# A four-stage transformer kernel on one core: five edits to its small elementwise steps and PSUM banks, with new order tables

## The chip, the cores and the metric

The kernel runs on one NeuronCore of a Trainium2 chip. A core has five engines with a queue each: PE (TensorE, matrix products; its weight loads are shown apart as PEld), DVE (VectorE), ACT (ScalarE), POOL (GpSimd) and SP, which here only issues DMAs. PE writes to PSUM, eight banks of 128 x 512 float32 values; DVE and ACT read PSUM and SBUF; POOL is used here on SBUF alone. The metric is device time in microseconds (us) of one execution, the median of several runs. Each engine works through its own instructions strictly in order and waits on semaphores, so an instruction that waits holds up all that stand behind it on that engine.

## The reference, cut to what matters

The input x is 16 blocks (batch elements) of 256 tokens by 128 features, with a context of 64 tokens per block. Four layers follow each other, each as x = x + tanh(gate) * layer(layernorm(x)):

```python
x = x + tanh(g_xattn[0]) * cross_attention_0(layernorm(x), ctx)   # 16 heads of 8, causal and padding masks
x = x + tanh(g_ffn[0])   * local_ffn(layernorm(x))                # 2 deep: windowed attention (8 heads of 64,
                                                                  # l2-normed q and k, rotary) and a gated MLP of 341
x = x + tanh(g_xattn[1]) * cross_attention_1(layernorm(x), ctx)   # 16 heads of 8, biases, padding mask
x = x + tanh(g_ffn[1])   * experts(layernorm(x))                  # 8 experts of width 128 or 256, top 2 by sigmoid
```

In the windowed attention the score of query i with key j is divided by both norms; the softmax subtracts the row maximum. In the experts every expert is computed for every token, and y = sum over e of comb[e] * y_e, with comb zero but for the best two. All is float32 but some masks.

## The kernel before

**Stages.** The program has three parts. `cross(0)` runs the first cross-attention over blocks 0 to 15, together with one-time preparation (transposing weights, keys and values of the context, masks). `local_ffn` runs for each depth l = 0, 1 the windowed attention over all blocks and then the gated MLP (GLU) over all blocks. `cross(1)` and `experts` run last, the experts beginning while the second cross-attention drains. A block is two tiles of 128 tokens; steps with a digit (top0, top1) are done once per tile, j = 0, 1.

**What sets the order.** Each stream is a table of steps (CROSS_STEPS, LOCAL_STEPS and so on), one line per step: name, lag in blocks, engine, cost, steps it needs, PSUM bank or buffer it takes and who gives that back. `timetable` (L337) walks the streams with the costs and emits one global order, which is then each engine's fixed order; earlier streams have priority. The costs are only the planner's; the chip follows the order at its own speed. A class of banks can have several homes: BIG means any of BIG0, BIG1, BIG2 (two banks each), while M and O are one bank each (`anywhere`, L1672).

**Cross-attention, one block.** DVE takes the statistics (`stat`), POOL the inverse root (`rstd`), DVE an offset -mean*rstd (`offset`, L926), POOL applies both (`apply`, L932). PE then turns the result (`turn`, bank M), makes the query (`query`, M), the scores (`score`, BIG); DVE takes row maxima (`top`) and splits them into bf16 parts (`parts`); PE turns those (`mturn`, M), makes the transposed scores (`score_t`, BIG); ACT does the exponentials (`exp`); PE mixes values (`mix`, bank O, L1103); ACT and DVE form the inverse sums (`log`, `inverse`, `refine`) and `share`, which gives O back; PE projects (`project`, M) and DVE adds to x (`add`, L1146), which gives M back.

**Windowed attention, one tile.** PE: `hturn` (bank VB), `qk` (QK, L1254), `value` (VB). ACT squares, DVE does `sin`, `cos` (both L1268, from PSUM) and `sums`. POOL: `clip`, `rotate` (two adds, L1302 and L1303), `norm` (four small operations), `scale` (L1330), `share` (L1400). PE turns q and k (bank TR), scores (bank SC, one tile at a time); DVE `top` takes the negated row maxima (L1373) and multiplies them by the query norms (L1378, 128 x 8); ACT `exp` does eight activations with that as bias (L1387) and gives SC back; DVE `total`, POOL `share`, PE `pturn` and `mix`. In layer 0 a further stream, `first`, normalizes blocks 2 to 15 with the same stat, rstd, offset, apply (writing y_sb) beside the attention.

**Experts, one block.** PE makes hidden units in three parts (`hid0` to `hid2`, L1623), ACT relu and square, PE the outputs of all 8 experts for one tile of tokens, `out0` and `out1` (L1645, 24 matmul records each, one BIG home each). DVE `sum` (L1653) adds the eight weighted outputs one after the other into x_sb, which gives the BIG home back, and SP stores the tile.

**Start.** Weights 0 (Wk), 1 (Wq), 2 (Wv), 3 (Wo) of the first cross-attention come by DMA, 0 and 1 on ACT's queue, 2 and 3 on SP's (L478 to L496). `wturn0` turns 0 and 1, `wturn1` turns 2 and 3 (L693).

Of the kernel before, what the change touches and what calls it, by code (L numbers as in the profile page):

```python
# [12 lines left out]
BF16 = mybir.dt.bfloat16  # L13
# [27 lines left out]
rstd 3 POOL 1.03 stat  # L41
mix 5 PE 1.8 exp0,exp1,vals O:share
query 2 PE 0.6 turn_out M:query_out
score_t 4 PE 1.2 mturn_out,query_out,keys BIG:exp0 BIG:exp1
share 6 DVE 0.43 refine oT:project
turn_out 3 ACT 0.38 turn xnT:query
log 6 ACT 0.38 mix
stat 0 DVE 0.92 - sm:apply
top0 3 DVE 1.2 score
project 6 PE 0.5 share M:add  # L50
query_out 3 ACT 0.39 query QT:score+score_t
inverse 6 ACT 0.38 log
top1 3 DVE 1.2 score,top0
parts 3 DVE 0.9 top0,top1 mp:mturn
add 6 DVE 0.48 project
exp0 5 ACT 1.08 score_t pT:mix
vals 5 POOL 0.32 - V:mix
apply 3 POOL 1.02 offset xn:turn
mturn 3 PE 0.25 parts M:mturn_out
offset 0 DVE 0.16 rstd  # L60
exp1 5 ACT 1.08 score_t,exp0
score 2 PE 1.25 query_out,keys BIG:top0 BIG:top1
turn 1 PE 0.4 apply M:turn_out
mturn_out 4 ACT 0.38 mturn mT:score_t
refine 5 DVE 0.84 inverse
keys 4 POOL 0.6 - Kd:score+score_t
# [3 lines left out]
inverse 6 ACT 0.38 log  # L70
score 6 PE 1.25 query_out,keys BIG:top0 BIG:top1
apply 1 POOL 1.02 offset xn:turn
stat 3 DVE 0.92 - sm:apply
turn 5 PE 0.4 apply M:turn_out
top0 6 DVE 1.2 score
exp0 5 ACT 1.08 score_t pT:mix
mturn_out 4 ACT 0.38 mturn mT:score_t
exp1 5 ACT 1.08 score_t,exp0
mix 8 PE 1.8 exp0,exp1,vals O:share
rstd 0 POOL 1.03 stat  # L80
top1 6 DVE 1.2 score,top0
parts 6 DVE 0.9 top0,top1 mp:mturn
keys 0 POOL 0.6 - Kd:score+score_t
query 5 PE 0.6 turn_out M:query_out
offset 4 DVE 0.16 rstd
add 9 DVE 0.48 project
turn_out 2 ACT 0.38 turn xnT:query
score_t 7 PE 1.2 mturn_out,query_out,keys BIG:exp0 BIG:exp1
refine 8 DVE 0.84 inverse
share 8 DVE 0.43 refine oT:project  # L90
log 5 ACT 0.38 mix
vals 2 POOL 0.32 - V:mix
project 9 PE 0.5 share M:add
query_out 2 ACT 0.39 query QT:score+score_t
mturn 6 PE 0.25 parts M:mturn_out
# [3 lines left out]
hid2 4 PE 1.88 turn_out,hid1 BIG:relu2  # L99
stat 4 DVE 0.92 -  # L100
hid0 3 PE 1.88 turn_out BIG:relu0
prob 8 ACT 0.22 router
rstd 0 POOL 0.95 stat
apply 0 POOL 0.9 offset exn:turn
relu1 7 ACT 1.06 hid1,relu0
out0 5 PE 2.9 square0,square1,square2 BIG:sum0
turn_out 6 ACT 0.38 turn exnT:hid2+router
square0 7 ACT 1.04 relu0
sum1 8 DVE 1.95 out1,route
router 4 PE 0.45 turn_out O:prob  # L110
relu2 7 ACT 1.06 hid2,relu1
sum0 7 DVE 1.95 out0,route
out1 5 PE 2.9 square0,square1,square2 BIG:sum1
square2 7 ACT 1.04 relu2
square1 7 ACT 1.04 relu1
offset 4 DVE 0.16 rstd
route 6 DVE 2.7 prob cb:sum0+sum1
hid1 3 PE 1.88 turn_out,hid0 BIG:relu1
relu0 6 ACT 1.06 hid0 h:out0+out1
turn 2 PE 0.44 apply M:turn_out  # L120
# [3 lines left out]
FIRST_STEPS = """  # L124
vals_out1 8 DVE 0.7 vals1
wturn_out1 4 ACT 0.38 wturn1
wturn1 4 PE 0.4 wload1 BIG:wturn_out1
vals2 8 PE 1.0 vals1,cdup1 BIG:vals_out2
dve 2 LD 1.4 -
vals_out2 9 DVE 0.7 vals2  # L130
wturn_out0 1 ACT 0.38 wturn0
unit 6 ACT 1.6 narrow
mload0 4 LM 5.0 -
cdup1 3 DVE 0.69 cturn1
pturn 5 PE 0.3 pens BIG:pturn_out
cdup0 4 DVE 0.69 cturn0
keys1 8 PE 0.95 cturn_out1 BIG:keys_out1
pool 8 LP 4.6 -
narrow 2 DVE 0.21 dve
cload0 0 LC 5.0 -  # L140
heads 1 DVE 0.62 dve
gates 5 ACT 0.3 act
nload 2 LN 8.0 -
act 9 LA 3.2 -
cturn1 1 PE 0.7 cload1 BIG:cturn_out1+cdup1
cturn_out1 5 ACT 0.61 cturn1
vals1 5 PE 1.0 vals0 BIG:vals_out1
xload0 3 LX 4.1 -
keys0 4 PE 1.7 wturn_out0,cturn_out0 BIG:keys_out0
wturn0 0 PE 0.8 wload0 BIG:wturn_out0  # L150
vals_out3 8 DVE 0.7 vals3
cload1 1 LC 2.2 cload0
cturn_out0 1 ACT 0.61 cturn0
part 2 DVE 0.55 dve
mload1 5 LM 6.0 mload0
pturn_out 5 DVE 0.2 pturn
late 2 DVE 2.0 pool
vals0 4 PE 1.1 wturn_out1,cdup0 BIG:vals_out0
keys_out0 5 ACT 0.61 keys0
wload0 3 LW 5.0 -  # L160
xload1 7 LX 1.5 xload0
wload1 6 LW 2.6 wload0
fill1 6 DVE 0.65 mload1,fill0
sels 3 DVE 0.28 heads
cturn0 0 PE 1.0 cload0 BIG:cturn_out0+cdup0
fill0 3 DVE 0.28 part,mload0
pens 4 DVE 0.7 nload
vals3 8 PE 1.0 vals2 BIG:vals_out3
keys_out1 9 ACT 0.61 keys1
vals_out0 4 DVE 0.7 vals0  # L170
# [3 lines left out]
keys1 1 PE 0.95 wturn_out BIG:keys_out1  # L174
vals_out0 6 DVE 0.7 vals0
bias 3 DVE 0.25 cols_out
vals1 4 PE 0.98 wturn_out BIG:vals_out1
wturn_out 4 ACT 0.62 wturn
rw_out 7 DVE 0.2 rw
cols_out 1 DVE 0.35 cols  # L180
cols 0 PE 0.15 - BIG:cols_out
vals_out3 2 DVE 0.7 vals3
vals0 4 PE 0.98 wturn_out BIG:vals_out0
rw 6 PE 0.15 - BIG:rw_out
keys_out1 1 DVE 0.75 keys1,cols_out
bo 2 PE 0.4 bias,wturn_out BIG:bo_out
vals_out1 4 DVE 0.7 vals1
keys_out0 8 DVE 0.75 keys0,cols_out
bo_out 4 DVE 0.25 bo
keys0 7 PE 0.95 wturn_out BIG:keys_out0  # L190
vals_out2 8 DVE 0.7 vals2
vals3 1 PE 0.98 wturn_out BIG:vals_out3
vals2 7 PE 0.98 wturn_out BIG:vals_out2
wturn 0 PE 0.6 - BIG:wturn_out
# [3 lines left out]
tab1 2 DVE 0.5 -  # L198
local2 7 POOL 0.65 -
tab2 8 DVE 0.5 -  # L200
seen 0 DVE 1.0 -
fill 0 DVE 1.2 -
local0 1 POOL 0.98 -
tab3 3 DVE 0.5 -
local1 8 POOL 0.65 -
local3 3 POOL 0.8 -
tab0 0 DVE 0.5 -
# [3 lines left out]
stat 0 DVE 0.92 -  # L211
rstd 0 POOL 0.95 stat
offset 1 DVE 0.16 rstd
apply 1 POOL 0.9 offset
# [9 lines left out]
norm0 3 POOL 0.87 root0  # L224
mix0 5 PE 1.07 pturn_out0,dma0 OB:mix_out0
qk1 2 PE 1.75 hout QK:square1+sin1+cos1
hout 0 ACT 0.78 hturn hb:qk0+qk1+value0+value1
sin1 2 DVE 1.21 qk1 u:rotate1
value0 3 PE 0.911 hout VB:value_out0
pturn0 4 PE 1 share0 TR:pturn_out0  # L230
share1 5 POOL 1.9 total1
mix1 5 PE 1.07 pturn_out1,dma1,dma0 OB:mix_out1
pturn_out1 4 ACT 1.02 pturn1 pT:mix1
mix_out0 4 ACT 0.62 mix0 oT:project
value_out0 3 DVE 0.7 value0 v:mix0+mix1
exp1 3 ACT 2.6 top1 pr:pturn1
total1 4 DVE 1.4 exp1
top0 3 DVE 1.4 score0,norm0
score0 3 PE 1.24 turn_out0 SC:exp0+top0
cos1 2 DVE 1.21 qk1 qn:turn1  # L240
root0 1 ACT 0.45 clip0
pturn_out0 3 ACT 1.02 pturn0 pT:mix0
dma1 7 DMA1 2.5 value_out1
sums1 2 DVE 1.22 square1
scale0 3 POOL 1.05 rotate0,norm0
clip1 3 POOL 0.27 sums1
square1 1 ACT 1.04 qk1 sq:sums1
turn1 3 PE 0.995 scale1 TR:turn_out1
mix_out1 4 ACT 0.62 mix1,mix_out0
rotate1 3 POOL 2.56 sin1,cos1  # L250
value1 3 PE 0.911 hout VB:value_out1
value_out1 3 DVE 0.7 value1
share0 4 POOL 1.9 total0
turn_out1 2 ACT 1.02 turn1
add 5 DVE 0.42 project
project 5 PE 1.69 mix_out0,mix_out1 OB:add
exp0 2 ACT 2.6 top0 pr:pturn0
total0 3 DVE 1.4 exp0
sin0 1 DVE 1.21 qk0 u:rotate0
cos0 1 DVE 1.21 qk0 qn:turn0  # L260
qk0 1 PE 1.75 hout QK:square0+sin0+cos0
turn0 2 PE 0.995 scale0 TR:turn_out0
square0 0 ACT 1.04 qk0 sq:sums0
norm1 3 POOL 0.87 root1
turn_out0 1 ACT 1.02 turn0 qT:score0+score1
scale1 3 POOL 1.05 rotate1,norm1
hturn 0 PE 0.3 - VB:hout
clip0 2 POOL 0.27 sums0
top1 3 DVE 1.4 score1,norm1
score1 3 PE 1.24 turn_out1,turn_out0 SC:exp1+top1  # L270
pturn1 4 PE 1 share1 TR:pturn_out1
root1 1 ACT 0.45 clip1
sums0 1 DVE 1.22 square0
dma0 0 DMA0 2.5 value_out0
rotate0 2 POOL 2.56 sin0,cos0
"""
GLU_STEPS = """
up0 1 PE 0.96 affine A:gate0+gate1
gelu2 2 ACT 0.47 up2,gelu0
bias 6 POOL 0.5 shift  # L280
shift 5 DMA2 2.8 - hg:apply
up1 1 PE 0.96 affine,up0
gate2 4 DVE 0.48 gelu2,gate0
gelu0 1 ACT 0.47 up0 hh:down
rstd 3 POOL 0.95 stat
stat 0 DVE 0.92 shift
gate0 3 DVE 0.48 gelu0
gelu1 1 ACT 0.47 up1,gelu0
out 4 DVE 0.48 down,bias
gate1 3 DVE 0.48 gelu1,gate0  # L290
down 2 PE 1.45 gate0,gate1,gate2
nturn 0 PE 0.44 apply N:affine
affine 0 ACT 0.5 nturn hnT:up0+up1+up2
apply 0 DVE 0.6 rstd hn:nturn
up2 1 PE 0.95 affine B:out
"""
LAST_GLU_STEPS = """
gate2 7 DVE 0.48 gelu2,gate0
apply 4 DVE 0.6 rstd hn:nturn
rstd 7 POOL 0.95 stat  # L300
shift 0 DMA3 2.8 - hg:apply
up0 4 PE 0.96 affine A:gate0+gate1
gate0 6 DVE 0.48 gelu0
back 8 DVE 0.35 out
bias 8 POOL 0.5 shift
gelu2 4 ACT 0.47 up2,gelu0
down 5 PE 1.45 gate0,gate1,gate2
up1 4 PE 0.96 affine,up0
out 7 DVE 0.48 down,bias
up2 4 PE 0.95 affine B:out  # L310
stat 3 DVE 0.92 shift
affine 2 ACT 0.5 nturn hnT:up0+up1+up2
gelu0 3 ACT 0.47 up0 hh:down
nturn 2 PE 0.44 apply N:affine
gelu1 3 ACT 0.47 up1,gelu0
gate1 6 DVE 0.48 gelu1,gate0
"""

LOGS, GELUS = "natural_log_exp_and_others", "gelu_and_others"

LOCAL_ROOM = dict(
    sq=1, u=2, qn=2, pr=2, pT=2, oT=2, qT=2, v=3, hb=3, hg=2, hn=2, hnT=2, hh=2,
    QK=1, SC=1, TR=1, VB=1, OB=1,
)
CROSS_ROOM = dict(
# [1443 lines left out]
```

## Time and profile before

| | |
|---|---|
| median of 3 runs | 1169.5 us (1165.39 to 1172.19) |
| the profiled execution | 1167.54 us, of which the span from first to last instruction is 1165.8 |
| granted TensorE clock | 0.986 of full speed |
| busy: PE, DVE, ACT, POOL | 1071.5, 938.5, 747.2, 631.9 us |
| HBM read, written | 9.46 MB, 2.10 MB |

By stage, from the trace's stretches (us busy in the stretch):

| stretch, us | what runs | length | PE | DVE | ACT | POOL |
|---|---|---|---|---|---|---|
| 30 to 147 | cross-attention 0 | 117 | 106.58 | 92.03 | 59.06 | 41.64 |
| 147 to 210 | windowed attention 0 fills | 63 | 45.94 | 51.68 | 37.04 | 48.58 |
| 210 to 390 | windowed attention 0 | 180 | 177.73 | 171.13 | 155.07 | 161.59 |
| 390 to 545 | its end, GLU 0, attention 1 fills | 155 | 135.69 | 111.16 | 89.27 | 75.65 |
| 545 to 750 | windowed attention 1 | 205 | 204.61 | 190.75 | 180.27 | 169.44 |
| 750 to 870 | its end, GLU 1, cross-attention 1 fills | 120 | 104.57 | 82.64 | 51.35 | 47.09 |
| 870 to 962 | cross-attention 1 | 92 | 82.75 | 75.51 | 55.12 | 48.65 |
| 962 to 1157.1 | experts | 195.1 | 194.83 | 138.65 | 108.54 | 24.46 |

How to read it: where PE is busy for all of a stretch, only less PE work or a faster PE shortens it; where PE has gaps, the waits say who closed each gap last. A busy engine is not proof of a bound, since a stretched instruction counts as busy too.

### The profile page before, as it was taken

Reading aid. Unit: us, or ns where it says so; the run is one execution under the profiler, and the core shown is the slowest. Engines: PE = TensorE matmul, PEld = TensorE weight load, DVE = VectorE, ACT = ScalarE, POOL = GpSimd, SP = SyncE. Lnnn points to the kernel's source line nnn. Section 1 sums busy time; section 2 is a strip of 40 time slices with the busy share of each in tenths; the row PEclk is TensorE's granted clock in tenths of the full one; section 3 lists DMA queues with packets and bytes.
Section 4 is the critical chain, followed back from the end, with each engine's and each line's share of the span. In section 5 each row is a group of like instructions: output and inputs, shape, how many; then the busy total and the mean of one; then the engine's idle time right before and its main releaser. Section 6 shows DMA issues by size and latency. Waiting matters only on the chain.

```text
span 1165.8 us, 29177 instructions
## 1 busy us (share of the span) xinstructions
PE 1071.5 (92%) x11648; PEld 802.7 (69%) x11648; DVE 938.5 (81%) x2088; ACT 747.2 (64%) x1465; POOL 631.9 (54%) x1047
## 2 busy tenths in 40 slices
PE   6999967999999989988999999979979999999997
PEld 4555625777777767855777777768745557999996
DVE  6887669999999965669999999857857884777777
ACT  3555437888888863458888888853336557555552
POOL 4453068999988843338888888733345460111110
PEclk9999979999999999999999999999989999999999
DMA  6400000111101111101111111111100000000000
GB/s 175 153 3 2 2 9 20 29 29 24 29 20 29 29 40 25 24 1 28 29 29 29 24 29 25 35 31 25 23 1 2 2 2 2 12 13 12 13 12 17
DMA packets 42740, 30.21 MB, mean 26 GB/s; under 512 B 21546, under 2 KB 35564, under 8 KB 42604
## 3 DMA queue, kind: packets, MB, share of 16 engines
q1 hardware_dynamic: 41260, 27.69, 9.5%
q8 instruction: 92, 1.51, 0.6%
q10 hardware_dynamic: 1344, 0.66, 0.2%
q14 instruction: 44, 0.36, 0.1%
HBM read 9.46 MB, written 2.10 MB: 10 GB/s over the span
## 4 chain that ended last, share of the span: by engine, by line
PE 64%; DVE 10%; DMA 4%; ACT 3%; issue 2%; SPq 2%; POOL 1%; DVEq 0%; POOLq 0%; ACTq 0%
PE QK L1257 9%; PE e_y L1645 7%; PE e_h_ps L1623 7%; PE OB L1417 5%; DMA gbuf<-y_sb 4%; PE TR L1405 4%; PE SC L1364 4%; PE TR L1336 4%; PE VB L1287 4%; PE OB L1436 3%; PE Ag L1515 3%; PE po L1111 2%; DVE qn L1268 2%; PE Bg L1515 2%; PE SC L1351 2%
## 5 line engine op out<-in xcount | busy, mean ns | idle before, releaser
L1387 ACT ACTIVATE pr<-SC,mx,rn 128x128 f32<-128x128 f32 x512 | 185.6, 469 | 23.5 <-DVE mx L1378 18.8
L1257 PE MATMUL QK<-wqkv,hbuf 128*128 128x512 f32 x256 | 129.4, 629 | 23.7 <-DVE qn L1268 22.8
L1400 POOL TENSOR_TENSOR pr<-pr,rs 128x1024 f32<-128x1024 f32 x64 | 121.5, 1899 | 10.5 <-DVE rs L1395 9.4
L1653 DVE SCALAR_TENSOR_TENSOR x_sb<-e_y,e_comb,x_sb 128x128 f32<-128x128 f32 x256 | 89.1, 349 | 21.6 <-PE e_y L1645 13.7
L1635 ACT ACTIVATE e_h<-e_h_ps 128x1024 f32<-128x1024 f32 x48 | 49.2, 1025 | 77.2 <-PE e_y L1645 61.8
L1268 DVE TENSOR_TENSOR u<-QK,tab 128x1024 f32<-128x1024 f32 x64 | 77.5, 1211 | 23.0 <-ACT sq L1265 13.8
L1645 PE MATMUL e_y<-mw,e_h 128*128 128x128 f32 x768 | 91.8, 277 | 0.0
L1623 PE MATMUL e_h_ps<-e_xnT,mw 128*128 128x256 f32 x384 | 89.8, 383 | 0.3
L1645 PEld LDWEIGHTS e_y<-mw,e_h 128*128 128x128 f32 x768 | 89.2, 192 | 0.7
L1257 PEld LDWEIGHTS QK<-wqkv,hbuf 128*128 128x128 f32 x256 | 44.4, 193 | 64.8 <-issue 43.9
L1373 DVE TENSOR_REDUCE mx<-SC 128x8 f32<-128x1024 f32 x64 | 77.5, 1212 | 12.1 <-PE SC L1364 12.1
L1036 DVE TENSOR_REDUCE nm<-sc 128x16 f32<-128x1024 f32 x64 | 74.8, 1210 | 14.0 <-PE sc L1027 13.8
L1302 POOL TENSOR_TENSOR qn<-qn,u 128x512 f32<-128x512 f32 x64 | 81.7, 1276 | 5.1
L1265 ACT ACTIVATE sq<-QK 128x1024 f32<-128x1024 f32 x64 | 65.7, 1026 | 26.3 <-ACT pr L1387 11.4
L1394 DVE TENSOR_REDUCE rs<-pr 128x8 f32<-128x1024 f32 x64 | 77.4, 1210 | 5.9 <-ACT pr L1387 4.1
L1303 POOL TENSOR_TENSOR qn<-qn,u 128x512 f32<-128x512 f32 x64 | 81.8, 1278 | 0.0
L1098 ACT ACTIVATE xpT<-sT,penT 128x1024 f32<-128x1024 f32 x64 | 69.5, 1114 | 17.5 <-PE sT L1088 17.4
L1268 DVE TENSOR_TENSOR qn<-QK,tab 128x1024 f32<-128x1024 f32 x64 | 77.6, 1213 | 1.1 <-ACT sq L1265 1.1
L1408 ACT COPY pT<-TR 128x1024 f32<-128x1024 f32 x64 | 64.4, 1006 | 21.6 <-PE TR L1405 21.6
L1623 PEld LDWEIGHTS e_h_ps<-e_xnT,mw 128*128 128x128 f32 x384 | 70.4, 190 | 10.9 <-DVE x_sb L1653 2.7
L1339 ACT COPY qkbuf<-TR 128x1024 f32<-128x1024 f32 x64 | 64.8, 1012 | 19.7 <-PE TR L1336 19.6
L1282 DVE TENSOR_REDUCE ss<-sq 128x16 f32<-128x1024 f32 x64 | 77.1, 1205 | 0.0
(213 smaller groups left out, 2629.1 us busy)
## 6 DMA issues: line engine op xcount, KB each, us to landing
vbuf<-vbuf SPq DMA_DIRECT2D x96, 128.0 KB
gbuf<-y_sb SPq DMA_DIRECT2D x32, 64.0 KB
out_dram<-x_sb SPq DMA_DIRECT2D x32, 64.0 KB
gbuf<-y_sb SPq DMA_DIRECT2D x32, 63.5 KB
wqkv<-in_L_ffn_wqkv_dram SPq DMA_DIRECT2D x2, 768.0 KB
mw<-in_L_ffn_w_dram SPq DMA_DIRECT2D x2, 768.0 KB
w<-in_L_ffn_w_dram SPq DMA_DIRECT2D x2, 341.0 KB
x_sb<-in_x_dram SPq DMA_DIRECT2D x1, 640.0 KB
```

The source lines that it names most:

```text
L1257: nc.tensor.matmul(ps[:, 512 * j : 512 * j + 512], lhsT=hbuf[b % 3][:, t * P : (t + 1) * P], rhs=wqkv[:, l, 512 * j : 512 * j + 512], star ...
L1268: nc.vector.tensor_tensor(work(tag, b, t, [P, 2, LH, LD], 2, wp), live["QK", b, t].rearrange("p (q h d) -> p q h d", q=2, h=LH), tab[:, l, ...
L1282: nc.vector.tensor_reduce(ss, live["sq", b, t].rearrange("p (g d) -> p g d", d=LD), AX.X, ALU.add)
L1302: nc.gpsimd.tensor_add(qg[:, :, 0:32], qg[:, :, 0:32], ug[:, :, 32:64])
L1303: nc.gpsimd.tensor_add(qg[:, :, 32:64], qg[:, :, 32:64], ug[:, :, 0:32])
L1373: nc.vector.tensor_reduce(mx, live["SC", b, t].rearrange("p (g c) -> p g c", c=P), AX.X, ALU.max, negate=True,)
L1387: nc.scalar.activation(pr[:, g, :], live["SC", b, t][:, g * P : (g + 1) * P], AF.Exp, bias=live["mx", b, t][:, g : g + 1], scale=live["rn" ...
L1394: nc.vector.tensor_reduce(rs, live["pr", b, t], AX.X, ALU.add)
L1400: nc.gpsimd.tensor_tensor(pr, pr, rs, ALU.mult)
L1623: nc.tensor.matmul(ps[:, c * S : (c + 1) * S], lhsT=mw1[:, (4 * j + c) * P : (4 * j + c + 1) * P], rhs=live["xnT", b], start=True, stop=True,)
L1645: nc.tensor.matmul(y[:, e * D : (e + 1) * D], lhsT=live["h", b][:, c, t * P : (t + 1) * P], rhs=mw2[:, c, :], start=(c == cs[0]), stop=(c ...
L1653: nc.vector.scalar_tensor_tensor(xt, live[f"y{t}", b][:, e * D : (e + 1) * D], live["comb", b][:, t, e : e + 1], xt, ALU.mult, ALU.add,)
```

## The change

Five edits, and new tables for all streams.

1. **Maxima.** The multiplication of the row maxima by the norms leaves `top` on DVE and becomes a step of its own on POOL, `bound`; `exp` now needs `bound`.
2. **LayerNorm.** The `offset` step goes in all streams; `apply` on POOL computes (x - mean) * rstd in one operation from the two columns.
3. **Banks.** In cross-attention and experts, each use of M or of O may take either of the two.
4. **Experts.** `out` is split by halves of four experts (`out0`, `out1` for the first tile of tokens, `out2`, `out3` for the second). DVE `weigh` multiplies four outputs by their weights in one operation into SBUF; POOL `gather` adds them up in three additions, the last into x_sb.
5. **Start.** `wturn` has three steps: weights 0 and 1, weight 2, weight 3. Weight 3 is loaded after blocks 4 to 6 of x instead of before.

The tables list the steps in other orders with other lags and some other costs. Core of the diff:

```diff
 NORM_STEPS = """
-stat 0 DVE 0.92 -
-rstd 0 POOL 0.95 stat
-offset 1 DVE 0.16 rstd
-apply 1 POOL 0.9 offset
+stat 0 DVE 0.92 - nsm:apply
+rstd 0 POOL 1.02 stat
+apply 1 POOL 0.9 rstd
...
-top0 3 DVE 1.4 score0,norm0
-exp0 2 ACT 2.6 top0 pr:pturn0
+top0 3 DVE 1.24 score0
+bound0 3 POOL 0.3 top0,norm0
+exp0 2 ACT 2.9 bound0 pr:pturn0
...
+    load_x(8, 14)
     load_weight(nc.sync, 3)
-    for lo, hi in ((8, 14), (14, 22), (22, 32)):
+    for lo, hi in ((14, 22), (22, 32)):
...
-            turn_weights(2 * j, 2, acc(f"wT{j}", home))
+            turn_weights(*((0, 2), (2, 1), (3, 1))[j], acc(f"wT{j}", home))
...
                 nc.gpsimd.tensor_scalar(
-                    xn[:, t, :], x[:, t, :], live["rstd", b][:, t : t + 1],
-                    live["off", b][:, t : t + 1], ALU.mult, ALU.add,
+                    xn[:, t, :], x[:, t, :], live["mv", b][:, t, 0:1],
+                    live["rstd", b][:, t : t + 1], ALU.subtract, ALU.mult,
                 )
...
-        def turn_(b, _):
-            turn(work("xnT_ps", b, [P, 512], 1, pp, tag="M"), live["xn", b])
+        def turn_(b, _, home):
+            turn(work("xnT_ps", b, [P, 512], 1, pp, tag=home), live["xn", b])
...
-            nc.vector.tensor_tensor(
+        def bound(b, t):
+
+            mx = live["mx", b, t]
+            nc.gpsimd.tensor_tensor(
                 mx.rearrange("p (u r) -> p u r", u=2), mx.rearrange("p (u r) -> p u r", u=2),
                 live["rn", b, t][:, 0:LH].rearrange("p (r u) -> p u r", u=2), ALU.mult,
             )
...
-        def out_(b, t, home):
-            y = work(f"y{t}", b, [P, 1024], 1, pp, tag=home)
-            for e in range(E):
+        def out_(b, j, home=None):
+
+            t, half = j // 2, j % 2
+            if half == 0:
+                work(f"y{t}", b, [P, 1024], 1, pp, tag=home)
+            for e in range(4 * half, 4 * half + 4):
...
-                nc.vector.scalar_tensor_tensor(
-                    xt, live[f"y{t}", b][:, e * D : (e + 1) * D], live["comb", b][:, t, e : e + 1],
-                    xt, ALU.mult, ALU.add,
-                )
-            nc.sync.dma_start(out_v[:, 2 * b + t, :], xt)
+        def weigh(b, j):
+            t, half = j // 2, j % 2
+            nc.vector.tensor_tensor(
+                work(f"w{j}", b, [P, 4, D], 4, wp, tag="e_w"),
+                live[f"y{t}", b][:, 512 * half : 512 * half + 512]
+                .rearrange("p (e d) -> p e d", e=4),
+                live["comb", b][:, t, 4 * half : 4 * half + 4].unsqueeze(2)
+                .to_broadcast([P, 4, D]), ALU.mult,
+            )
+
+        def gather(b, j):
+            w, xt = live[f"w{j}", b], x_sb[:, 2 * b + j // 2, :]
+            nc.gpsimd.tensor_add(w[:, 0:2, :], w[:, 0:2, :], w[:, 2:4, :])
+            nc.gpsimd.tensor_add(w[:, 0, :], w[:, 0, :], w[:, 1, :])
+            nc.gpsimd.tensor_add(xt, xt, w[:, 0, :])
+            if j % 2:
+                nc.sync.dma_start(out_v[:, 2 * b + j // 2, :], xt)
...
-    anywhere = lambda r, b: accs if r == "BIG" else (r,)
+    anywhere = lambda r, b: accs if r == "BIG" else ("M", "O") if r in ("M", "O") else (r,)
```

## The prediction

> **What bounds the kernel now.** All sums stand against the profiled execution: 1167.54 us, a span of 1165.8 with 1.8 around it; the median of the three runs, 1169.5, is 2.0 above it. I read the clock first (0.986, so a lost clock explains nothing), then the busy shares and slices.
>
> ```profile
> PE 1071.5 (92%) x11648; PEld 802.7 (69%) x11648; DVE 938.5 (81%) x2088; ACT 747.2 (64%) x1465; POOL 631.9 (54%) x1047
> ...
> PE   6999967999999989988999999979979999999997
> ```
>
> PE has 92%, so at most 1165.8 - 1071.5 = 94 us can go without less PE work, and no edit removes a matrix product. The rest is where those 94 us lie. I cut the span into stretches (columns: length, then PE, PEld, DVE, ACT, POOL busy):
>
> ```profile
> 90.00:120.00 30.00, 27.70 (x465) 16.61 (x460) 22.66 (x57) 15.35 (x29) 9.42 (x21) 1.00 0.01 2
> 240.00:270.00 30.00, 29.23 (x378) 21.50 (x379) 29.41 (x41) 25.04 (x58) 27.84 (x41) 1.00 0.08 19
> 600.00:630.00 30.00, 30.00 (x390) 22.35 (x388) 27.84 (x33) 26.19 (x57) 24.99 (x35) 1.00 0.12 28
> 1020.00:1050.00 30.00, 29.96 (x214) 28.07 (x214) 22.62 (x90) 15.53 (x20) 4.56 (x10) 1.00 0.04 12
> ```
>
> Windowed attention 1 (third row) and the experts (fourth) have no PE gap: in their steady part the edits can only lose. PE idles elsewhere, by the stretches of the table above: 11.2 us in the first 30, 10.4 in cross-attention 0, 17.1 at 147 to 210, 2.3 at 210 to 390, 19.3 at 390 to 545, 15.4 at 750 to 870, 9.3 in cross-attention 1, 8.7 after the last product. The waits of PE (us, times, longest) name the closers in the stretches 0 to 30, 30 to 147, 870 to 962 and 390 to 545, in this order:
>
> ```profile
> PE p_wT L653 <- DMA w_nat<-in_L_xattn_Wo_dram: 5.1, 1, 5.1
> ```
> ```profile
> PE mT_ps L1058 <- DVE x_sb L1148: 7.3, 13, 0.6
> ```
> ```profile
> PE mT_ps L1058 <- DVE x_sb L1148: 6.3, 11, 0.6
> ```
> ```profile
> PE QK L1257 <- DVE qn L1268: 5.1, 3, 2.0
> PE Bg L1515 <- DVE y_sb L1552: 4.7, 12, 1.5
> ```
>
> **Start: -4.5 (0 to -5.1).** In the timeline PE stands from 7.85 to 12.94 for Wo:
>
> ```profile
> 12.94 0.47 PE L653 MATMUL p_wT<-ident,w_nat 128*128 128x128 f32 x1 [5.09 <-DMA w_nat<-in_L_xattn_Wo_dram]
> ```
>
> Wv, in the same step, was there: it turned at 7.43. In the changed order the turn of Wo is its own step, behind the first scores; Wo is needed only by the first `project`. Next late is ACT's chain of copies, from context copy (7.19) over eight query copies (2.50), xnT 0.38, KT 0.59, wT 0.25, a context copy 0.59 and QT 0.39: 11.9. The keys and turns on PE behind that put the first score near 14, against 18.91; 4.5 of 5.1 is kept. If the three context products wait for something else, nothing is gained.
>
> **Cross-attention 0: -5.6 (0 to -7.3).** `mturn` needs M, which the `add` of an older block holds, 0.58 us in nearly every block; blocks (from `add` to `add`) are 7.24 apart. PE's own work from start to start is score_t 1.47, project 0.71, mturn 0.21, score 1.41, turn 0.37, mix 1.86, query 0.63 = 6.66, and 7.24 - 6.66 = 0.58 is that wait. With two homes for M, mturn takes the other bank. In the changed order a PE turn comes to the bank that `mix` held until DVE's `share`; that loop is turn 0.37, score 1.41, top 2.32, parts 1.07, refine 0.9, share 0.42 and 0.17 between engines = 6.66, just PE's floor. Two loops of one length rub; I leave 0.15 per block and take 0.43 x 13 = 5.6.
>
> **Cross-attention 1: -6.0 (0 to -6.3).** The same wait, 11 times. The floor is 6.74 - 0.57 = 6.17, the loop here, without parts and with a score of 1.2, is 5.4 and stays hidden. The experts' first turn also comes two blocks earlier among PE's instructions, which fills the drain.
>
> **Windowed attention 0: +1.1 (-3 to +12).** Here POOL sets the pace (27.84 of 30, second row, and it runs `first` besides). One tile on POOL, start to start: clip 0.36, rotate 2.46, norm 1.22, scale 1.04, share 1.87 = 6.95; a block's LayerNorm is 1.1 + 0.93 = 2.0. Before, 13 LayerNorms stood beside ten blocks' rotates: 2 x 6.95 + 1.3 x 2.0 = 16.5, and `hturn` shows 16.42 (178.06 to 325.86 in nine periods). The new step `bound` is not in this trace on POOL. Nearest is L1319, a product of like kind, twice as wide:
>
> ```profile
> L1319 POOL TENSOR_TENSOR ss<-ss,rn 128x16 f32<-128x16 f32 x64 | 14.3, 224 | 7.8 <-ACT rn L1314 7.8
> ```
>
> I take 0.22 + 0.08 of gap = 0.30; 0.72 + 0.08 as for L924's power of two columns is the upper end, 0.15 (about its free time on DVE) the lower. In the changed order one LayerNorm stands beside each of blocks 1 to 11: 2 x 7.25 + 2.0 = 16.5, 0.1 above before for eleven blocks: +1.1. At 0.80 it is 17.5, 1.1 more for eleven blocks: +12; at 0.15, 0.3 less per block, -2 to -3.
>
> **Windowed attention 1: 0 (0 to +3).** POOL needs 2 x 7.25 = 14.5 of PE's 15.74 per block. Following one block through the new order, `bound` is done 1.1 us before `exp` needs it and SC is given back 0.25 to 0.7 us before its next score; that cover is thin (see the rivals).
>
> **Fills, drains, GLU: -3.3 (-12 to +5).** DVE operations with two SBUF inputs stretch beside POOL (L1378: min/median/max in ns):
>
> ```profile
> L1378 DVE TENSOR_TENSOR mx<-mx,rn x64: 166/821/1678, 174.0 to 770.0; 128x8 f32<-128x8 f32 x64
> ```
>
> A product of 128 x 8 elements takes 166 ns alone, 1678 beside a long POOL operation. One case, with what stood behind it:
>
> ```profile
> 189.69 1.90 POOL L1400 TENSOR_TENSOR pr<-pr,rs 128x1024 f32<-128x1024 f32 x1
> ...
> 190.22 1.39 DVE L1378 TENSOR_TENSOR mx<-mx,rn 128x8 f32<-128x8 f32 x1
> 191.54 1.21 DVE L1268 TENSOR_TENSOR qn<-QK,tab 128x1024 f32<-128x1024 f32 x1
> ...
> 192.80 1.98 PE L1257 MATMUL QK<-wqkv,hbuf 128*128 128x512 f32 x4 [1.96 <-DVE qn L1268]
> ```
>
> The small product ends with POOL's (191.6), the rotary product behind it starts only then, and PE waits for that. The Trainium skill says the same of the pair (SBUF — State Buffer, SBUF: two separate sides): the shared port is an exclusive lock for a whole instruction, held by whichever began first. L1378 and the offset (L927, up to 1.22) leave DVE. Between 176 and 196 their excess over a free one is 4.0 us with PE waiting for qn; some of it would have been waited for anyway, so 2.5, and 0.8 of GLU 0's fill. The bounds are a quarter of the 50 us of PE idle in fills and drains, and as much lost as the new orders could add by one late block.
>
> Against moving `bound` to POOL speaks another page (GPSIMD Engine Reference, 4.1 Engine selection): elementwise products there are about twice as slow as on VectorE; by that factor on DVE's free 166 ns, `bound` would be an estimated 0.33, and the sum the same within 1 us.
>
> **Experts, steady: 0; tail: +0.8 (-3.2 to +4).** 768 records in `out` before and after. DVE falls from 16 x 0.38 = 6.1 us a block to 4 x 0.69 (row of p_V by umask, 128 x 512, 689 ns) = 2.8. POOL gets four `gather`: 0.73 for 256 columns,
>
> ```profile
> L1539 POOL TENSOR_TENSOR y_sb<-y_sb,b 128x256 f32<-128x256 f32 x32 | 23.1, 726 | 0.0
> ```
>
> and, by the slope to L1302's 1276 at 512, 0.45 each for two of 128: with gaps 1.8. Four and a LayerNorm are 9.2 of 11.5 us: covered. At the end PE stops at 1157.15 and DVE's last sums end at 1163.2, 6.0 later. After: the last four `out` pairs take 2.78 each, the eight gathers behind them 14.4 us from 7.6 before PE's end, so POOL ends 6.8 after it. If a gather costs 1.3, POOL keeps up and ends 2.8 after: -3.2; at 2.2, +4.
>
> POOL's waits for the offset (33.1 and 77.1 us in all) were its own idle time: 0.
>
> **Sum:** -4.5 - 5.6 - 6.0 + 1.1 - 3.3 + 0.8 = -17.5; 1167.5 - 17.5 = **1150.0**, its own range 1143 to 1157. The bounds together reach further, but are not met at once.
>
> **Rivals.** (A) *The banks only move the wait*, from mturn to turn or query: for it, the loop of 6.66 equals the floor in cross-attention 0; against it, cross-attention 1 has 0.7 to spare. Then 11.6 comes back: 1161.5. Chance 0.14. (B) *The new orders also fill the drains*: PE idles some 50 us there, and the experts' turn moves as needed; against it, these are chains through three engines. A third of it gone is -16: 1134. Chance 0.13. (C) *Slower: `bound` queues on POOL* behind rotate (2.46) or share (1.87), so `exp` starts late, SC comes back late and PE waits in both attentions, where it has no gap now. It decides from about 1.3 us of delay per tile; at 1.9, the length of share, 0.6 x 64 tiles = 38: 1150 + 38 = 1188. For it: DVE did the product in 0.82 at the median, and POOL has 93% in layer 0. Against it: in the new order `bound` stands between short steps. Chance 0.12. Forecast: 0.61.
>
> **How the numbers follow.** The range 1136 to 1165 holds the forecast's cases, A and half of B. About 0.5%, 5.8 us, can be told from no change: faster is the forecast, B and half of A; A's other half is the same; C is slower. 0.80, 0.08, 0.12.
>
> **What would show it.** Right: no wait of mturn for `add`; blocks 6.7 to 6.85 apart in cross-attention 0, 6.2 to 6.3 in 1; the first score near 14; `bound` at 0.2 to 0.3; `hturn` 16.5 apart in layer 0, 15.74 in layer 1; the last gather 6.8 after PE. Wrong: a new wait of turn for the `share` with the old 7.24; PE waits for SC beyond 1.3 us per tile; a POOL share near 100% in the attentions; gathers late enough for PE to wait for BIG.

## The result and the profile after

The changed kernel takes 1189.0 us (median of 4, 1188.1 to 1189.8), the kernel before 1168.1 on the same chip: 1.0172 times as long, interval 1.0148 to 1.0197. The forecast was 1150, faster. The first lines of the page of after:

```profile
PE 1081.7 (91%) x11648; PEld 803.1 (68%) x11648; DVE 850.2 (72%) x1768; ACT 747.2 (63%) x1466; POOL 793.3 (67%) x1303
...
PE   7999868999999988888999999978879999999996
```

DVE lost 88 us of work as the change meant it to, POOL gained 161, and PE, which has the same products, has 106 us without work instead of 94. The stretches again (same columns; the last row is a second one of the experts):

```profile
90.00:120.00 30.00, 29.75 (x482) 17.91 (x477) 23.49 (x54) 15.77 (x30) 10.88 (x20) 1.00 0.01 2
240.00:270.00 30.00, 28.82 (x382) 21.03 (x381) 25.60 (x32) 25.04 (x53) 27.43 (x42) 1.00 0.11 24
600.00:630.00 30.00, 29.74 (x382) 21.10 (x381) 25.64 (x28) 25.45 (x57) 24.95 (x35) 1.00 0.11 23
1060.00:1090.00 30.00, 28.48 (x197) 26.56 (x196) 14.39 (x59) 16.63 (x22) 23.58 (x42) 1.00 0.04 11
```

Cross-attention 0 is nearly full now; the three that were full or nearly so have gaps. By stage, from the timelines of PE (starts of the first score and the first hturn, ends of the last products; the forecast's -3.3 for fills stands as -2.5 in attention 0 and -0.8 in GLU 0):

| stage | before | forecast | after |
|---|---|---|---|
| to the first score | 18.9 | -4.5 | 15.6 (-3.3) |
| cross-attention 0, to the first hturn | 127.0 | -5.6 | 122.6 (-4.3) |
| attention 0, to its last projection | 294.6 | -1.4 | 303.6 (+9.0) |
| GLU 0 | 79.8 | -0.8 | 84.7 (+4.9) |
| attention 1 | 267.8 | 0 | 275.9 (+8.1) |
| GLU 1 | 69.4 | 0 | 75.1 (+5.8) |
| cross-attention 1, experts | 299.7 | -6.0 | 300.7 (+1.1) |
| behind PE's last product | 8.6 | +0.8 | 9.8 (+1.1) |

Most of the gains of the start and of cross-attention 0 came, and they were gone by the end of attention 0.

### The profile page after: what moved, and what is told of

It is laid out like the page before. It is cut to its first block, busy times and chain, and to the rows that moved or that the text cites. A ratio compares the mean times of both kernels' runs of the same rounds, so it can differ in the third digit from the quotient of the medians.

```text
span 1188.1 us, 29185 instructions
## 1 busy us (share of the span) xinstructions
PE 1081.7 (91%) x11648; PEld 803.1 (68%) x11648; DVE 850.2 (72%) x1768; ACT 747.2 (63%) x1466; POOL 793.3 (67%) x1303
## 4 chain that ended last, share of the span: by engine, by line
PE 32%; DVE 11%; POOL 5%; DMA 3%; issue 1%; ACT 1%; SPq 1%; DVEq 0%; POOLq 0%; ACTq 0%
PE e_y L1656 7%; PE e_h_ps L1631 7%; DMA gbuf<-y_sb 3%; POOL pr L1408 2%; PE po L1116 2%; PE QK L1262 2%; PE OB L1444 2%; PE TR L1341 2%; PE SC L1369 2%; DVE qn L1273 2%; DVE rs L1402 1%; DVE mx L1378 1%; PE TR L1413 1%; PE VB L1292 1%; PE sc L1032 1%
## 5 line engine op out<-in xcount | busy, mean ns | idle before, releaser
L1262 PE MATMUL QK<-wqkv,hbuf 128*128 128x512 f32 x256 | 126.6, 618 | 15.3 <-DVE qn L1273 14.5
L1664 DVE TENSOR_TENSOR e_w<-e_y,e_comb 128x512 f32<-128x512 f32 x64 | 42.6, 689 | 84.1 <-PE e_y L1656 81.3
L1262 PEld LDWEIGHTS QK<-wqkv,hbuf 128*128 128x128 f32 x256 | 47.4, 196 | 65.6 <-issue 52.3
L1425 PEld LDWEIGHTS OB<-pT,vbuf 128*64 128x64 f32 x2048 | 65.9, 139 | 31.9 <-issue 26.1
L1341 PEld LDWEIGHTS TR<-ident,qn 128*128 128x128 f32 x512 | 60.8, 143 | 36.0 <-issue 32.8
L1674 POOL TENSOR_TENSOR e_w<-e_w 128x256 f32<-128x256 f32 x64 | 46.4, 726 | 57.3 <-DVE e_w L1664 57.3
L1413 PE MATMUL TR<-ident,pr 128*128 128x128 f32 x512 | 69.2, 278 | 15.7 <-POOL pr L1408 12.4
```

Source lines behind the costliest of these rows:

```text
L1262: nc.tensor.matmul(ps[:, 512 * j : 512 * j + 512], lhsT=hbuf[b % 3][:, t * P : (t + 1) * P], rhs=wqkv[:, l, 512 * j : 512 * j + 512], star ...
L1341: nc.tensor.transpose(ps[:, i * P : (i + 1) * P], qf[:, i * P : (i + 1) * P], ident)
L1413: nc.tensor.transpose(ps[:, g * P : (g + 1) * P], live["pr", b, t][:, g, :], ident)
```

## The experiments

Ratios are to the kernel before, run beside each. Stage times come from one profiled execution of each kernel, which can lie some us from its median (at most 4.7, old_mid_pool), so a stage that differs by 2 or 3 us decides little. "Eleven blocks" are the starts of hturn from block 4 to 15: 177.6 us before and 184.6 after in attention 0, 173.3 (15.74 a block) and 177.4 (16.09) in attention 1.

**Orders or product?** The product goes back to DVE, once with the old tables in the middle part (attention, both GLUs) and once with all the new ones:

```diff
-        def bound(b, t):
-            nc.gpsimd.tensor_tensor(mx, mx, rn, ALU.mult)
+            nc.vector.tensor_tensor(mx, mx, rn, ALU.mult)   # again in top
```

> The changed kernel with two things set back in the middle part: the tables of windowed attention and of both GLUs are those of before, and the product of maxima and norms is again done by DVE in top. Start, cross-attentions, banks, LayerNorm and experts stay changed. In the profiles the middle part (first hturn to the last product of GLU 1) took 711.6 us before and 739.3 after. Theory 1, the new orders of the middle part cost the time: 711 to 713 again, attention-1 blocks 15.74 apart, 1189 - 27 = 1162 in all. Theory 2, the LayerNorm without an offset, which stays, costs it: 735 or more, 1185 or more.

> The changed kernel with all new tables, but the product of maxima and norms done by DVE in top, and the step bound left out. Theory 1 (orders): the middle part stays at 735 to 745 us, attention-1 blocks stay 16.09 apart or more, 1186 to 1194 in all. Theory 3, rival C of the forecast (the product on POOL starts exp late or holds POOL up): the middle part falls back to some 712 and the time to 1162.

Old orders: 1168.1, ratio 0.9999 (0.9981 to 1.0018), 6 more than theory 1's 1162; GLU 0 79.8, attention 1 268.6, GLU 1 70.0, as before within 1 us, but attention 0 298.0, 3.4 more than before. New orders with DVE's product: 1201.4, 1.0278 (1.0249 to 1.0306), 12 us slower than the changed kernel and above either theory. So the new tables of the middle part cost most of the time, and the product on POOL gains in them. The step itself, and under it who waited for it, after:

```profile
L1386 POOL TENSOR_TENSOR mx<-mx,rn x64: 196/205/223, 167.0 to 782.9; 128x8 f32<-128x8 f32 x64
...
  ACT pr L1395: 2.0, 4
```

0.205 us each, and exp waited 2.0 us in all for 64 of them.

**The experts' new wait.** Before, PE waited for nothing in the steady experts; after, 0.51 us a block:

```profile
1086.16 1.05 PE L1656 MATMUL e_y<-mw,e_h 128*128 128x128 f32 x8
1087.05 0.51 PE L1586 MATMUL e_pl<-rwT,e_xnT 128*128 128x8 f32 x4
1088.06 1.16 PE L1656 MATMUL e_y<-mw,e_h 128*128 128x128 f32 x8 [0.51 <-DVE e_w L1664]
```
```profile
1087.32 0.69 DVE L1664 TENSOR_TENSOR e_w<-e_y,e_comb 128x512 f32<-128x512 f32 x1 [1.42 <-PE e_y L1656]
```

The four products into a tile's first half end, DVE weighs them (1087.32 to 1088.01), and only then PE goes on with the second half of the same tile. In the written order weigh stands between the two; where it doesn't (the other tile of each block), PE has no such wait. Here and below, behind(x, y, ...) moves a block's step x to just behind its step y in the written order, where the steps named after them still follow.

```diff
+        behind("weigh0", "out1", "gather0")
+        behind("weigh2", "out3", "gather2")
```

> The changed kernel with one thing moved in the written order: the first weigh of a tile stands behind the tile's second out instead of ahead of it, so that no product into the tile's second half is written behind a read of its first half. Theory (the wait of 0.5 us per block that the experts' products have for weigh, blocks 11.88 apart, is an order between write and read of one tile, not a lack of a bank): the wait goes, blocks 11.49 apart, 12 blocks, -5: 1184. Rival (the bank is really late): the wait stays or moves to the next out, 1189.

1181.8, 1.0113 (1.0086 to 1.0140). The wait is gone, the blocks are 11.21 apart (11.88 after, 11.49 before), and the stage is 7.5 us shorter.

**The loop of attention 1.** Its blocks are 16.09 apart, and the waits of PE name nobody between 560 and 700. First one exchange in the table:

```diff
-score1 3 PE 1.24 turn_out1,turn_out0 SC:exp1+top1
 hturn 0 PE 0.3 - VB:hout
+score1 3 PE 1.24 turn_out1,turn_out0 SC:exp1+top1
```

> The changed kernel with one exchange in its attention table: hturn stands ahead of score1 instead of behind it, so that score1 and mix0 are neighbours on PE. Theory 1a (a change of PE between 128-row products and the 64-row products of score and mix costs time, by the starts of neighbours some 0.09 us per change, and DVE's rotary product waits 1.21 us per block for hturn): attention-1 blocks 15.74 to 15.92 apart instead of 16.09, 13 blocks a layer: -4 to -9, 1180 to 1185. Theory 1b (the blocks are 16.09 apart because the loop over share sets the pace): no block shorter than 16.05, 1189.

1189.6, 1.0183 (1.0155 to 1.0212), and 16.09 as in the changed kernel: PE's own work does not set it, theory 1a falls. The timeline of after (PE, DVE, ACT, POOL, in order of time):

```profile
615.46 1.88 PE L1262 MATMUL QK<-wqkv,hbuf 128*128 128x512 f32 x4
617.45 1.23 DVE L1273 TENSOR_TENSOR u<-QK,tab 128x1024 f32<-128x1024 f32 x1 [0.24 <-PE QK L1262]
618.77 1.02 ACT L1270 ACTIVATE sq<-QK 128x1024 f32<-128x1024 f32 x1 [0.99 <-DVE u L1273]
619.88 1.23 DVE L1273 TENSOR_TENSOR qn<-QK,tab 128x1024 f32<-128x1024 f32 x1 [1.21 <-PE VB L909]
622.15 1.21 DVE L1402 TENSOR_REDUCE rs<-pr 128x8 f32<-128x1024 f32 x1
623.75 1.90 POOL L1408 TENSOR_TENSOR pr<-pr,rs 128x1024 f32<-128x1024 f32 x1 [1.22 <-DVE rs L1403]
625.70 1.09 PE L1413 MATMUL TR<-ident,pr 128*128 128x128 f32 x8
```

Three operations read the bank QK: DVE's sin (u), ACT's square (sq), DVE's cos (qn). They only read, yet each begins when the one before has ended: sq 0.09 behind u, qn 0.09 behind sq. (The name in qn's bracket is the last event seen, hturn; with hturn moved it reads sq.) Behind qn stand maxima, sums, then POOL's share and PE's turn of it. From that turn to the next sin are 7.85 us (609.60 to 617.45), from sin to share 6.30, from share to the turn 1.95: 16.10. These rows are a block's first tile. Before, the tables wrote its square ahead of both of DVE's reads (for the second tile it stood between them before, too):

```profile
608.02 1.03 ACT L1265 ACTIVATE sq<-QK 128x1024 f32<-128x1024 f32 x1 [0.33 <-ACT pr L1387]
609.23 1.19 DVE L1268 TENSOR_TENSOR u<-QK,tab 128x1024 f32<-128x1024 f32 x1
610.33 1.22 DVE L1268 TENSOR_TENSOR qn<-QK,tab 128x1024 f32<-128x1024 f32 x1
```

The Trainium skill (PSUM — Partial Sum Buffer, "PSUM bank collisions raise a hardware error") tells of such an order: the compiler's scheduler adds a dependency between two engines' instructions that touch one bank and quadrant (32 partitions), "reads and writes alike". The trace agrees: sq starts 0.09 behind u, and its bracket names u.

```diff
+        behind("square0", "cos0", "sums0")
+        behind("gate0", "gelu1", "down", "gate1", "gate2")
```

> The kernel of the hturn exchange, with three reorderings in the written order: square0 stands behind cos0 (not between sin0 and cos0, which all read the bank QK), gate0 behind gelu1 (both read bank A) in both GLUs, and each first weigh behind the tile's second out. Theory 4 (what ACT and DVE do to one tile of PSUM is done in written order, even where they only read, and the new tables wrote ACT's reader between two of DVE's, so that the loop QK, sin, square, cos, maxima, sums, share, pturn is 16.09 long): attention-1 blocks 15.75 to 15.8 apart, 4 to 5 us less; GLU 0 back from 84.7 to 80 or 81 us, GLU 1 from 75 to between 70 and 74; with 7 for weigh 1167 to 1176 in all. Rival (POOL's share or its own queue sets the 16.09): attention stays at 16.09, 1175 to 1182.

1199.1, 1.0245 (1.0227 to 1.0263), where 1167 to 1176 was expected. Both attentions went to 17.02 a block, GLU 0 only to 83.0, GLU 1 to 74.1. The timeline of this kernel, ACT and then PE:

```profile
663.28 1.02 ACT L1282 ACTIVATE sq<-QK 128x1024 f32<-128x1024 f32 x1 [2.21 <-DVE qn L1285]
664.21 1.01 ACT L1356 COPY qkbuf<-TR 128x1024 f32<-128x1024 f32 x1
```
```profile
665.36 1.06 PE L1425 MATMUL TR<-ident,pr 128*128 128x128 f32 x8 [1.24 <-ACT qkbuf L1356]
```

Square waits 2.2 us a block for qn, the copy of the next turned tile queues behind it on ACT, TR comes back late and PE waits for that. Each reader still waits for the one written ahead of it; the new place was bad. One more move, past those copies, with hturn moved and weigh and gate back where they were:

```diff
+   square0(b) behind the last of cos0(b), turn_out0(b - 1), hout(b + 1)
```

> The changed kernel with hturn ahead of score1, and square0 in the written order behind cos0, turn_out0 and hout (in the kernel before this one it stood only behind cos0 and held up turn_out0 behind it on ACT by its 2.2 us wait). Theory 4 (the loop QK, sin, square, cos, maxima, sums, share, pturn sets 16.09 since square is done between sin and cos): without square in it the loop is 1.2 us shorter, PE's own 15.77 decides: attention-1 blocks 15.75 to 15.8 apart, 4 us less in each attention at most, 1180 to 1185. Rival (the pace comes from ACT's or POOL's queue): 16.0 or more, 1187 or more.

1178.7, 1.0088 (1.0059 to 1.0116). Its timeline:

```profile
606.14 1.88 PE L1278 MATMUL QK<-wqkv,hbuf 128*128 128x512 f32 x4
608.13 1.23 DVE L1289 TENSOR_TENSOR u<-QK,tab 128x1024 f32<-128x1024 f32 x1 [0.24 <-PE QK L1278]
609.28 1.21 DVE L1289 TENSOR_TENSOR qn<-QK,tab 128x1024 f32<-128x1024 f32 x1
610.61 1.03 ACT L1286 ACTIVATE sq<-QK 128x1024 f32<-128x1024 f32 x1
613.14 1.90 POOL L1424 TENSOR_TENSOR pr<-pr,rs 128x1024 f32<-128x1024 f32 x1 [1.22 <-DVE rs L1419]
616.03 1.09 PE L1429 MATMUL TR<-ident,pr 128*128 128x128 f32 x8
```

From u to share are 5.01 instead of 6.30; share ends at 615.04, 1 us before PE wants it; the eleven blocks of attention 1 are 15.74 apart, all of them (173.1), and those of attention 0 take 181.0. Attention 1 as a whole is 270.9, 5.1 less than in the changed kernel; the 3.0 that it is still longer than before lie outside these blocks and stay open.

**The GLUs.** In the two table versions PE, ACT, POOL and the DMAs have one and the same order within each GLU; only DVE's differs: the statistics of the next block stand directly behind apply instead of one to three operations later. They need a DMA into the buffer (gbuf) that an earlier apply gave back. DVE's waits of the statistics (stg) in GLU 0, before and then after:

```profile
DVE stg L1478 <- DMA gbuf<-y_sb: 3.6, 10, 0.7
```
```profile
DVE stg L1486 <- DMA gbuf<-y_sb: 9.6, 10, 1.8
```

Gates (hhg) queue behind the waiting statistics, and PE waits for gates, again before and then after:

```profile
PE Bg L1544 <- DVE hhg L1533: 1.1, 1, 1.1
```
```profile
PE Bg L1552 <- DVE hhg L1541: 5.5, 6, 1.1
```

With the old tables the GLUs take 79.8 and 70.0 again (above), so DVE's order costs the time; that it does so through the DMA is read from these waits. The direct test of the DMA, a third buffer, was not run.

**What the parts are worth.** The middle part with its old tables (the norms' too), DVE's product and the moved weigh; then with bound on POOL; then with one bank each:

```diff
+bound0 4 POOL 0.3 top0,norm0                       # old_mid_pool
-anywhere = ... ("M", "O") if r in ("M", "O") else (r,)
+anywhere = ... (r,)                                # old_mid_one_bank
```

> The changed kernel with the middle part's tables of before (attention, both GLUs, and the norms' table too, whose offset line is now idle), the product of maxima and norms by DVE, and each first weigh behind the tile's second out. Theory: the gains of start, cross-attentions and experts stay (-7.6 at the first hturn, -6.4 from GLU 1 to the experts' end), the middle part is 711.6 again or a little less without the offset, the tail +1.1: 1168 - 13 = 1155, between 1153 and 1161. Rival (the stages pull on one another and gains are given back later): 1165 or more.

> The same kernel, but with the product as POOL's own step bound in the old attention table: bound0 behind rotate0 and norm0 of the next block, bound1 behind share0 and norm1. Rival C of the forecast (the step queues behind 2.46 of rotate or 1.87 of share, exp starts late, SC comes back late, PE waits): attention blocks 16.3 or more apart, +10 to +40 us beside the kernel with DVE's product. Against it (POOL has room, and the step takes DVE's stretched 0.82 away): within 2 us, or up to 5 less.

> The same kernel with DVE's product, and M and O again one bank each with fixed uses. The forecast's terms (0.43 x 13 and 6.0 by the second home): cross-attention 0 some 4 to 6 us longer, cross-attention 1 with the experts 4 to 6 longer, +8 to +12 in all; with orders made for two banks perhaps more. Rival A (the wait only moves): within 3 us.

1162.0 (0.9914, 0.9900 to 0.9929); 1164.1 (0.9934, 0.9918 to 0.9950); 1187.5 (1.0146, 1.0129 to 1.0162). The first was expected at 1155 and came out 1 us beyond its range; attention 0 kept 181.8 for eleven blocks, and attention 1 was 3.2 longer than before, nearly all of it outside its eleven blocks. Bound on POOL made the eleven blocks 187.3 in attention 0 and 173.2 in attention 1 (173.6 without): it costs where POOL sets the pace, and nothing in attention 1's blocks. Rival C's sign is there in attention 0, 17.0 a block against 16.5, but its 10 to 40 us in all are not. One bank cost 6.6 us in cross-attention 0 and 18 behind GLU 1, more than forecast, in orders made for two.

**The form of LayerNorm.** What kept attention 0 at 181.8 is in the groups of POOL, before and after:

```profile
L936 POOL TENSOR_SCALAR y_sb<-x_sb,n_rstd,n_off 128x128 f32<-128x128 f32 x32 | 14.1, 448 | 2.2 <-DVE n_off L927 2.2
```
```profile
L941 POOL TENSOR_SCALAR y_sb<-x_sb,n_mv,n_rstd 128x128 f32<-128x128 f32 x32 | 25.5, 803 | 0.0
```

The offset form back for blocks 2 to 15, in that kernel and in the changed one, and three other forms:

```diff
+  (x * rstd + off)            # old_mid_off, new_first_off: offset on DVE, as before
+  (x + mean) * rstd, x * rstd + mean, x * rstd - mean     # apply_forms
```

> The kernel with the middle part's tables of before, DVE's product and the moved weigh, and now also the LayerNorm of the norms beside attention 0 (blocks 2 to 15) as before: offset on DVE, then POOL multiplies and adds. In the changed kernel POOL's (x - mean) * rstd took 0.80 us for 128 x 128, the multiplication and addition of before 0.45, so 0.7 more a block on the engine that sets attention 0's pace. Theory 5 (this form of the operation costs attention 0 some 4 us, the only difference left there): attention 0 with its fill 294 to 295 us instead of 298.6, 4 less than the kernel without this, 1158. Rival (attention 0 varies by that much from run to run, or loses it to start times): no change, 1162.

> The changed kernel with nothing set back but that LayerNorm's form (offset on DVE, multiplication and addition on POOL) and the table line for it, for blocks 2 to 15 beside attention 0. Theory 5: 0.7 less on POOL per block, eleven blocks, attention 0 with its fill 4 to 8 us shorter than 303.6: 1181 to 1185. Rival: there PE waits for shares that come late through DVE's order, and POOL's time does not matter: 1187 to 1190.

> The changed kernel with three forms of POOL's normalizing operation on 128 x 128, to see what makes it 0.80 us; the values are then not LayerNorm's: in the cross-attentions (x + mean) * rstd, beside attention 0 x * rstd + mean, in the experts x * rstd - mean. If the subtraction is slow: 0.45, 0.45, 0.80. If it is the order, a multiplication last: 0.80, 0.45, 0.45. If it is reading the mean with its stride of two values: 0.80 in all three.

The three forms:

```profile
L946 POOL TENSOR_SCALAR xn<-x_sb,mv,rstd 128x128 f32<-128x128 f32 x64 | 28.2, 450 | 14.5 <-PE Bg L1554 14.2
L946 POOL TENSOR_SCALAR e_xn<-x_sb,e_rstd,e_mv 128x128 f32<-128x128 f32 x32 | 25.4, 802 | 5.2 <-PE e_xnT_ps L909 5.1
L946 POOL TENSOR_SCALAR y_sb<-x_sb,n_rstd,n_mv 128x128 f32<-128x128 f32 x32 | 14.2, 453 | 0.0
```

It is the subtraction: 0.80 in either place, 0.45 without. That kernel took 1177.8 in a single run, eleven blocks of attention 0 179.1. With the offset back and the old tables: 1156.1, ratio **0.9889** (0.9868 to 0.9910), 177.7 as before; it has the lowest median of the study. In the new tables the offset did not give the 1181 to 1185 expected: 1193.3, 1.0212 (1.0184 to 1.0239), eleven blocks 184.8 as without it. There the line for offset also moved the LayerNorms among the blocks (ten of them fall into the eleven instead of nine; periods of 16.46, then one of 19.04), so that run can't part the form from its place. Hence the same values without subtracting:

```diff
+            nc.vector.tensor_scalar_mul(ng, mean, -1.0)     # in stat
-  (x - mean) * rstd
+  (x + ng) * rstd
```

> The changed kernel with all its tables, but the mean negated on DVE in stat (128 x 2) and POOL adding it: (x + (-mean)) * rstd, the same values. Theory 5 (the subtraction on POOL, 0.80 against 0.45 us, sets attention 0's pace): attention 0 some 9 us shorter (294 to 297 instead of 303.6), cross-attention 1 with the experts 3 shorter, nothing elsewhere: 1189 - 11 = 1178. Rival (the gain seen with the other forms came of their other values or of chance): above 1185.

1191.0, 1.0189 (1.0165 to 1.0213), not the 1178 expected. Eleven blocks of attention 0 fell as expected, to 179.0. But cross-attention 0 took 126.9 instead of 122.6. The wait of turn for the bank that DVE's share gives back, after and with the negation:

```profile
PE xnT_ps L909 <- DVE oT L1139: 1.7, 5, 0.5
```
```profile
PE xnT_ps L909 <- DVE oT L1140: 4.4, 5, 1.9
```

The loss is not one of every block: from the sixth period on the blocks are 6.87 apart with the negation as without. The third to fifth periods hold 4.0 of it (7.89, 8.56 and 8.49 us instead of 7.18, 6.92 and 6.87); there DVE also does the statistics and negations of the stream `first` (n_mv, n_ng) between its steps for the cross-attention. Attention 0's fill was 1.3 longer. Cross-attention 1's first blocks went from 6.57 to 6.37, but from GLU 1 to PE's end nothing was won.

**All mended.** The changed kernel with square, hturn and weigh moved, the GLUs' old tables and the negated mean; and the negated mean in the old tables:

> The changed kernel with all that was found set right: the mean negated and added, hturn ahead of score1, square0 out of the loop, the GLUs' tables of before (which differ in DVE's order alone), the first weigh behind the second out. If the five causes are all there is and add up: attention 0 293 to 296, GLU 0 79.8, attention 1 268 to 270, GLU 1 70, cross-attention 1 and experts 290, start and cross-attention 0 as changed: 1150 to 1157. If one of them only hides another: 1162 or more.

> The middle part's tables of before with DVE's product and the moved weigh, and the negated mean added on POOL in all LayerNorms. Against the kernel with DVE's offset beside attention 0 (1156): the same there, and 2 to 3 us less in cross-attention 1 and the experts, 1153; against the kernel with the subtraction (1162): 8 to 9 less.

1160.8 (0.9915, 0.9893 to 0.9937) and 1157.9 (0.9907, 0.9888 to 0.9926), both 4 to 5 us above what was expected. The new orders mended: eleven blocks 174.4 and 173.1 (before 177.6 and 173.3), GLUs 77.0 and 68.4 (79.8 and 69.4), all at or below the kernel before; 28 us of the 39 between forecast and result are recovered, 4 are lost again in cross-attention 0 with the negation. Open are attention 0's fill (first hturn to block 4), 46 to 54 us among these kernels, and what attention 1 takes outside its eleven blocks (271.4 in all, before 267.8), by causes that I did not separate.

## Why the prediction was wrong

Some three quarters of its gains at the start and in cross-attention 0 came; it failed where it put 0 or a gain on the later stages that the new orders touched.

- **Start, -4.5**: -3.3. The wait for Wo went. What was late next was not ACT's chain alone: ahead of the first score PE also waited 1.2 us for DVE's mask piece and 0.4 for a first LayerNorm.
- **Cross-attention 0, -5.6**: -4.3. mturn no longer waits for add; the blocks are 6.87 apart against 6.81 forecast, and turn waits for share (1.7 us), the loop that was named as rubbing. **Cross-attention 1, -6.0, and experts, 0**: together +1.1. The first was 6.57 a block, not 6.17 (6.74 before); with the negated mean it is 6.37, so half of that miss goes with the slower LayerNorm. In the experts the step that failed is "768 records in out before and after": the same products, but a read written between two halves of one tile made PE wait, 0.67 a block (11.88 against 11.21). With weigh moved the two stages are 6.4 shorter than before. That this is near -6.0 is in part luck: 0.28 in each of the last ten blocks (11.49 to 11.21) is the experts' own, where the forecast had 0.
- **Attention 0, +1.1**: seven in eleven blocks. "A block's LayerNorm is 1.1 + 0.93 = 2.0" was taken from rows of multiplication and addition for an operation that the diff turns into a subtraction; it is 1.1 + 1.6. That is 5.5 of the 7.0 (new_negated, apply_forms); moving hturn and square is worth 3.6 (hturn alone 0.6), and everything mended 10.2. The other 2 of the +9.0 are the fill. The row that the prediction shows for "POOL sets the pace" has DVE at 29.41 and PE at 29.23 of 30, above POOL's 27.84; that POOL's time counts there is shown only by these runs.
- **Attention 1, 0**: the step that failed is "following one block through the new order": I followed bound and SC, and not the three readers of QK. Its blocks went to 16.09; moving square gives 15.74 again, and 5.1 of the 8.1. The two extra changes between 128- and 64-row products that I took for the cause after the result are not it.
- **Fills and GLU, -3.3**: the stretched DVE products did leave (0.82 at the median), but no run shows a gain in a fill from it: with the old tables attention 0's fill is 49.9 with the product on DVE and 49.2 with it on POOL. And I read GLU orders only for what the edits removed, not for DVE's place of the statistics; the GLUs got 10.7 longer.
- **Tail, +0.8**: +1.1. The last gather ended 7.2 us behind PE's last product, 6.8 forecast.
- **Rival C** had the time, 1188, and not the mechanism: its price was 0.6 us a tile for a late bound; ACT waited for bound 2.0 us in all, and taking it away cost 12. A right number is no proof of a cause. The Trainium skill's factor of two for POOL against DVE (GPSIMD Engine Reference, 4.1 Engine selection) is not what these 128 x 8 products show: 0.205 on POOL, 0.17 at the least and 0.18 at the median on DVE (new_order_dve). **Rival A**: no; mturn's wait went, 4.3 of the 5.6 came in cross-attention 0, and without the second home it is 6.6 longer, though in an order made for two. **Rival B**: GLUs and attentions got longer, not shorter. (By the prediction's own rule the chances of faster and same add up to 0.81 and 0.07, not 0.80 and 0.08.)

## What to carry to other kernels

When an order changes, follow every reader of a PSUM bank, and not only writers and readers: DVE and ACT take turns in written order, and a tile's second half waits for a read of its first half that is written ahead of it. Price an operation by a row of the same arithmetic, not only of the same shape. And compare each engine's order stage by stage, the ones that no edit touches first: with the middle part's old tables, its product and the LayerNorm beside attention 0 as before, and weigh moved, the other edits gave 1156 instead of 1189.

## What the runs showed of the hardware

POOL's (x - m) * r with columns takes 0.80 us for 128 x 128 float32, and x * r - m too; with an addition it is 0.45 (447 to 454 ns in the mean of these groups; one, xn of the kernel before, has 483). DVE's and ACT's reads of one PSUM bank ran one after the other, 0.09 to 0.12 us apart where nothing else held them up in the blocks shown after the change. PE ran the experts at 11.21 us a block with weigh moved, below the 11.49 that had seemed full before; the profile shows no wait of PE in either, and why the new order is faster stays open.
